# The slot table, the return of the first image and the opening of the scans in a four-layer network on one core

## The chip, the cores and the metric

The kernel runs on one core of a Trainium2 chip. A core has TensorE (PE; its weight loads are shown as PEld), VectorE (DVE), ScalarE (ACT), GpSimd (POOL) and SyncE (SP), which issues DMAs. The metric is the device time of one execution in microseconds (us); lower is better.

## The reference, cut to what matters

Four layers, each added to its input `x` (2 images of 128 channels, 56x56) after a group norm: agent attention, a 3x3 convolution, a mixture of experts over 2x2 patches, and a two-directional Mamba scan over the rows.

```
x = x + _L0_conv_ref(_gn(x), ...)      # attention
x = x + _L1_conv_ref(_gn(x), ...)      # 3x3 convolution
x = x + _L2_conv_ref(_gn(x), ...)      # experts
x = x + _L3_conv_ref(_gn(x), ...)      # scans
...
logits = xp @ router_w                  # xp: 1568 tokens of 512
topv, topi = jax.lax.top_k(softmax(logits), 2)
for e in range(8):
    val, g = jnp.split(xp @ w1[e], 2, axis=-1)
    out = out + gate[:, e:e+1] * ((val * sigmoid(g)) @ w2[e])
...
xc = silu(conv_b + causal conv of 4 taps)            # Mamba, each direction
dt = softplus(...); h = exp(dt * A) * h + dt * u * B; y = h . C
```

All data is float32.

## The kernel before

**Slot table.** Each token goes to two experts. The kernel sorts the 2 x 1568 pairs into tiles of 128 slots (`SLOTS`), each tile of one expert; up to 32 tiles (`TILES`) are possible, 25 are sure (`self.fewest`), and this input has 28. At the end of `route`, `inv` gets, for each slot and tile, the token and its share. It is one product over tokens: `is_slot` (112 tokens x 128 slots, 0 or 1) is the stationary side, `what` (112 tokens x 64: token and share for 32 tiles) the moving one; 14 token blocks for each of the two choices, 28 matmuls that add into one PSUM bank (L1292). DVE builds `is_slot` and `what` in two rooms that lie in buffers of the weights.

**Experts.** `run` (from L1315) loops over tiles. For tile j, SP reads the expert's number into a register (`expert`, L1324) and issues `w1` (4 MB, L1331) and `w2` (2 MB, L1336); each has two buffers. POOL gathers the tile's 128 tokens (`xr`, indirect DMA, L1306, four buffers). `up` transposes them on PE (`xr_ps`, L1354), DVE copies them to `xs_c` (L1356), and 64 matmuls (L1365) fill four banks `h_ps`, a quarter each; ACT takes the sigmoid (`sg`, L1375), DVE multiplies to `ht` (L1377). `down` of the tile before (8 matmuls `o_ps`, L1385, ACT's `ot`, L1388, and a DMA to `os`) follows `up`. A matmul of float32 shows as two records. Outside blocks of `manual_schedule` the framework's scheduler orders each engine's instructions by its own estimates; `issue_after(ins)` makes what the block issues on the engine of `ins` come after `ins`.

**Return of image 0.** Tiles 0 to 19 hold all of image 0 (`self.ahead` is 20). `arrive` is a generator: `combine` gathers, for each of 7 token blocks, two rows per token from `os` (`g0`, `g1`, L1306 again), DVE adds them (L1461), PE transposes the sum (`y_ps`, L1464), DVE adds it onto `x` (L1437) and takes statistics (L88); then come three stages of the group norm (L100, `gn_ps` L104 and L116) and the roots. `lead` blocks are gathered ahead. `run` calls `next(beside)` at tile 20 three times (`LEAD`), and from tile 21 on at every `spot()`, after each half of `up` and after each `down`; a `spot` holds PE's part behind the last matmul traced (`traced`). After tile 24 the rest of the generator runs, and then a `Switch` on the number of further tiles, here 3.

**Opening of the scans.** `mamba_pair` keeps its own order on all engines. An agenda books stages by steps; steps below 0 prepare direction f of block 0: `conv`, `silu`, `low`, `step`, `log`, `softplus`, `weigh`, `send_steps`. In the same steps the generator `second` brings image 1 back from all 28 tiles and takes its norm. Each `next` of it gathers one block and works on it at once (`lead` 0). Its PSUM banks are the wide ones of `dA` (`wide_bank`). Then come 448 units: ACT makes `dA` (L1876), POOL `dBu` (L1887), DVE scans (L1906), and DVE or POOL multiplies by C.

Of the kernel before, what the change touches and what calls it, by code (L numbers as in the profile page):

```python
# [8 lines left out]
F32 = mybir.dt.float32  # L9
# [1004 lines left out]
class PatchExperts:  # L1014
# [15 lines left out]
    def route(self, dram, wpool, conv):  # L1030
# [9 lines left out]
        with tc.tile_pool(name="l2_route", bufs=1) as one, tc.tile_pool(  # L1040
# [12 lines left out]
            four = one.tile([P, 32], F32, name="four")  # L1053
            nc.vector.tensor_reduce(four, net.ident.rearrange("p (q e) -> p e q", q=4), AX.X, ALU.add)
            shape = [T, nt, experts]

# [192 lines left out]
            self.slots = []  # L1249
            inv = ps.tile([P, 512], F32, name="inv", tag="tr")  # L1250
            rooms = [
# [3 lines left out]
            for n, room in enumerate(rooms):  # L1255
# [27 lines left out]
                for some in (range(per), range(per, nt)):  # L1283
                    ts = slice(some[0], some[-1] + 1)
                    nc.vector.tensor_tensor(
                        is_slot[:, ts, :],
                        slot_of.unsqueeze(1).to_broadcast([T, per, SLOTS]),
                        low[:, ts].unsqueeze(2).to_broadcast([T, per, SLOTS]),
                        ALU.is_equal,
                    )  # L1290
                    for t in some:
                        nc.tensor.matmul(  # L1292
                            inv[:, : 2 * TILES],
                            is_slot[:, t, :],
                            what[:, t].rearrange("t h j -> t (h j)"),
                            start=n == 0 and t == 0,
                            stop=n == 1 and t == nt - 1,
                        )

            self.whom = keep.tile([P, TILES], I32, name="whom")  # L1300
            nc.vector.tensor_copy(self.whom, inv[:, :TILES])
# [13 lines left out]
    def run(self, wpool, work, ps, beside):  # L1315
# [11 lines left out]
        downs = [wpool.tile([P, nj, 512], F32, name="w2", tag="w2") for _ in range(2)]  # L1327

        def up_weights(j, e):
            w1 = ups[j % 2]  # L1330
            nc.sync.dma_start(w1, w1s[e].rearrange("o c q f -> (o c) q f"))  # L1331
            return w1
# [5 lines left out]

        traced = [None]

        def spot():
            with net.tc.issue_after(traced[0]):
                next(beside, None)

# [5 lines left out]
        def up(j, w1, xr):  # L1350

            tp = ps.tile([P, 512], F32, name="xr_ps", tag="tr")
            for q in range(4):
                nc.tensor.transpose(tp[:, q * P : (q + 1) * P], xr[:, q * P : (q + 1) * P], net.ident)  # L1354
            xc = work.tile([P, 4, SLOTS], F32, name="xs_c", tag="xs_c")
            nc.vector.tensor_copy(xc.rearrange("c q s -> c (q s)"), tp)  # L1356
            ht = work.tile([P, nj, SLOTS], F32, name="ht", tag="ht")
            for c in range(2):
                parts = []
                for part in (1, 0):  # L1360
                    h_ps = ps.tile([P, 512], F32, name="h_ps", tag="h", bufs=4)
                    for i in range(4):
                        f0 = part * hidden + (4 * c + i) * P
                        for q in range(4):
                            mm = nc.tensor.matmul(  # L1365
                                h_ps[:, i * SLOTS : (i + 1) * SLOTS],
                                w1[:, q, f0 : f0 + P],
                                xc[:, q, :],
                                start=q == 0,
                                stop=q == 3,  # L1370
                            )
                    traced[0] = mm.ins
                    parts.append(h_ps)
                sg = work.tile([P, 4 * SLOTS], F32, name="sg", tag="sg")
                nc.scalar.activation(sg, parts[0], AF.Sigmoid)  # L1375
                to = ht[:, 4 * c : 4 * c + 4, :].rearrange("k j s -> k (j s)")
                nc.vector.tensor_mul(to, parts[1], sg)  # L1377
                if self.ahead + 1 < j + c < self.fewest + c:
                    spot()
            return ht  # L1380
# [13 lines left out]
        for j in range(self.fewest):  # L1394
            e = expert(j)
            w1, w2 = up_weights(j, e), down_weights(j, e)
            ht = up(j, w1, gather(j))
            if last is not None:
                down(*last)
            last = (j, ht, w2)  # L1400
            if j == self.ahead:
                for _ in range(LEAD):
                    next(beside)
            elif j > self.ahead:
                spot()
        for _ in beside:
# [75 lines left out]

LEAD = 3

# [95 lines left out]
def arrive(net, combine, b, gathered, bank, banks, pool, norms, lead=0):  # L1580
    nc = net.nc
    yield from combine(b, gathered, bank, lead)
    got = []
    for stage in net.norm_stages(b, banks, "mm", got.append):
        fetch = stage()
# [10 lines left out]
def mamba_pair(net, out, wts, combine, keep, norms):  # L1596
# [19 lines left out]
    with ExitStack() as ctx:  # L1616
# [15 lines left out]
        def wide_bank(name):  # L1632
            return ps.tile([P, 1024], F32, name=name, tag="dA", bufs=2)

        class Banks:
            def tile(self, shape, dtype, name, tag):
                return wide_bank(name)[:, :512]

# [100 lines left out]
        class Half:  # L1739
# [5 lines left out]

            def conv(self, m):
                w = self.w
# [11 lines left out]
                if m == 0:  # L1759
                    self.xc = work.tile([P, 2, BLK], F32, name="xc", tag=f"xc{w.d}", bufs=1 if w.d == "f" else 2)  # L1760
                return lambda: nc.scalar.activation(
                    self.xc[:, m, :], pm[:, :BLK], AF.Identity, bias=w.conv_b[:, m : m + 1]
                )

# [187 lines left out]
        for n, blk in enumerate(blocks):  # L1952
# [3 lines left out]
            if n == 0:  # L1956

                book(at + 1, blk.norm)
                book(at + 3, lambda f=f: f.conv(0))
                book(at + 4, lambda f=f: f.conv(1), tag="c")  # L1960
                book(at + 6, lambda f=f: silu(f, None))
                book(at + 7, f.low)
# [8 lines left out]
                for i, (h, m) in enumerate(((f, 0), (f, 1), (b, 0), (b, 1))):  # L1971
                    book((1, 4, 5, 13)[i], lambda h=h, m=m: h.gate(m))
                book(at + 17, lambda b=b: b.conv(0))
                book(at + 17, lambda b=b: b.conv(1), tag="c")
                book(at + 19, lambda b=b: silu(b, None))
                for m in range(2):
# [66 lines left out]
        with tc.manual_schedule(engines={E.PE, E.Activation, E.DVE, E.Pool, E.SP}):  # L2043
            nc.scalar.preload_act_table_set(EXP_LN)
            second = arrive(net, combine, 1, gathered, wide_bank, ps_of_norms, keep, norms)
            first = min(agenda)
            for step in range(first, 0):
                run(step)
                for _ in range((0, 0, 0, 2, 0, 1, 1, 0, 1, 1, 1, 1, 0, 1, 1, 1)[step - first] if step - first < 16 else 1):
                    next(second, None)  # L2050
                fetch(step + 1)
            for _ in second:
                pass
        with tc.manual_schedule(engines={E.PE, E.Activation, E.DVE, E.Pool, E.SP}):
# [5 lines left out]
            for n, (h, u) in enumerate(units):  # L2060
# [13 lines left out]
                if done:  # L2074
                    done.pop().close()
                waiting.append((h, u))

                quota = 0 if u == 3 and n > 3 else 2 if u == 7 and n > 7 else 1
# [125 lines left out]
```

## Time and profile before

| | |
|---|---|
| median of 3 runs | 3031.53 us (3031.18 to 3033.45) |
| the profiled execution | 3033.16 us, its span 3031.1 us |
| busy, share of the span | PE 89%, DVE 72%, ACT 61%, POOL 48% |
| attention and convolution | to about 1000 us |
| `inv` matmuls | 1011.82 to 1024.0 us |
| experts, first `h_ps` to last `ot` | 1036.2 to 1677.7 us |
| first scan | 1717.74 us |
| weights `w1` (4 MB), issue to landing | median 20.4 us, 12.5 to 23.1 |
| weights `w2` (2 MB), issue to landing | median 10.9 us, 9.3 to 30.0 |
| `os` written | 28 x 256 KB, median 7.9 us to landing |
| gathers (L1306), issue to landing | median 7.8 us, 3.3 to 14.0 |

A line of a timeline has the start, the duration, engine, source line, operation, what it writes and reads, and a count of instructions that follow each other; brackets hold the idle time of the engine before them and what ended it. "issue" is a wait for nothing that the profile names.

### The profile page before, as it was taken

The numbers are of one execution on the slowest core, as the hardware profiler recorded it, in microseconds if no ns is written. First come the engines' busy times: TensorE is split into PE (matmuls) and PEld (weight loads), VectorE is DVE, ScalarE is ACT, GpSimd is POOL, SyncE is SP. The second block draws the span as 40 slices with busy tenths as digits, with TensorE's granted clock in tenths as the row PEclk, the third lists the DMA queues.
The fourth block names the chain that finished last, engine by engine and source line by source line (L and its number), as shares of the span: only waits on it lengthen the run. The fifth ranks groups of instructions, "written<-read, shape, count | busy, mean of one in ns | idle before, by whom it ended". The sixth has DMA issues, their size and how long they took to land. (4 is left out here: it accounts for less than half of the span.)

```text
span 3031.1 us, 39355 instructions
## 1 busy us (share of the span) xinstructions
PE 2697.4 (89%) x14924; PEld 1283.4 (42%) x14924; DVE 2184.0 (72%) x1854; ACT 1853.7 (61%) x2944; POOL 1450.5 (48%) x801
## 2 busy tenths in 40 slices
PE   7999999999998799999898778888888888888874
PEld 3333333333335688788777323333333333233321
DVE  5978998999886301010120589999999999999996
ACT  5778788778751100000001488888888888888884
POOL 3000010010322100000100589999999999999995
PEclk9999999999999799999999799899899999999987
DMA  1000000000002668788875554465555565545460
GB/s 55 1 1 1 1 1 1 1 1 1 1 1 60 263 272 318 314 310 321 303 279 206 129 125 116 114 148 130 120 118 121 117 147 127 127 116 120 115 148 22
DMA packets 157934, 369.32 MB, mean 122 GB/s; under 512 B 25156, under 2 KB 114980, under 8 KB 154132
## 3 DMA queue, kind: packets, MB, share of 16 engines
q1 hardware_dynamic: 135744, 339.30, 37.5%
q0 software_dynamic: 5520, 15.62, 1.6%
q10 hardware_dynamic: 16452, 11.61, 1.2%
q8 instruction: 122, 2.00, 0.3%
q14 instruction: 96, 0.79, 0.1%
HBM read 297.89 MB, written 17.20 MB: 104 GB/s over the span
## 5 line engine op out<-in xcount | busy, mean ns | idle before, releaser
L1887 POOL TENSOR_TENSOR dBu<-dtu,Bs 128x896 f32<-128x896 f32 x448 | 921.3, 2094 | 14.4 <-DMA dtu<-sp_u 10.5
L1906 DVE TENSOR_TENSOR_SCAN h<-dA,dBu 128x896 f32<-128x896 f32 x448 | 882.3, 2009 | 28.2 <-ACT dA L1876 24.8
L620 ACT ACTIVATE ex<-sc 128x896 f32<-128x896 f32 (+1 forms) x700 | 602.6, 918 | 124.7 <-PE sc L617 113.4
L1928 PE MATMUL y<-h,both 128*64 128x448 f32 x1792 | 468.2, 615 | 82.2 <-POOL h L1915 74.9
L627 DVE TENSOR_TENSOR ex_sum<-ex_sum,ex 128x1792 f32<-128x1792 f32 (+1 forms) x238 | 492.6, 2070 | 35.3 <-ACT ex L620 21.3
L1365 PEld LDWEIGHTS h_ps<-xs_c,w 128*128 128x128 f32 x3584 | 406.5, 193 | 28.6 <-ACT ot L1388 15.4
L1365 PE MATMUL h_ps<-xs_c,w 128*128 128x128 f32 x3584 | 409.9, 277 | 9.0 <-issue 9.0
L617 PE MATMUL sc<-q,k 32*128 32x448 f32 (+1 forms) x2800 | 403.6, 587 | 3.6 <-ACT ex L620 2.9
L1917 DVE TENSOR_TENSOR h<-h,c_ps 128x1792 f32<-128x1792 f32 (+1 forms) x168 | 326.6, 1944 | 26.9 <-ACT c_ps L1894 10.1
L635 PE MATMUL av<-ex,va 128*32 128x448 f32 (+1 forms) x2800 | 334.3, 552 | 0.1
L582 POOL TENSOR_TENSOR a_e<-a_e,a_inv 112x784 f32<-112x784 f32 x14 | 41.6, 2973 | 584.0 <-ACT ex L620 394.5
L1377 DVE TENSOR_TENSOR ht<-h_ps,sg 128x512 f32<-128x512 f32 x56 | 38.5, 691 | 391.8 <-PE h_ps L1365 339.7
L1876 ACT ACTIVATE dA<-dt,f_A 128x448 f32<-128x448 f32 x448 | 282.7, 636 | 50.7 <-DVE h L1906 39.7
L1876 ACT ACTIVATE dA<-dt,b_A 128x448 f32<-128x448 f32 x448 | 282.8, 635 | 33.1 <-DVE h L1906 24.2
L1928 PEld LDWEIGHTS y<-h,both 128*64 128x64 f32 x1792 | 118.9, 147 | 354.8 <-issue 212.6
L1306 POOL DMA_INDIRECT xr<-xd,whom x28 | 28.1, 1004 | 493.3 <-PE xr_ps L1354 449.3
L1915 POOL TENSOR_TENSOR h<-h,Cs 128x1792 f32<-128x1792 f32 (+1 forms) x70 | 252.5, 3608 | 6.9 <-PE sp_ps L1841 3.4
L617 PEld LDWEIGHTS sc<-q,k 32*128 32x128 f32 (+1 forms) x2800 | 137.7, 181 | 230.1 <-issue 132.5
L1375 ACT ACTIVATE sg<-h_ps 128x512 f32<-128x512 f32 x56 | 33.4, 597 | 310.0 <-PE h_ps L1365 309.9
L1385 PE MATMUL o_ps<-w,ht 128*128 128x512 f32 x448 | 204.4, 601 | 1.2 <-DVE ht L1377 1.2
L1388 ACT ACTIVATE ot<-o_ps,share 128x512 f32<-128x512 f32 x28 | 19.2, 687 | 255.5 <-PE o_ps L1385 255.5
L625 DVE TENSOR_TENSOR ex_sum<-ex 128x1792 f32<-128x1792 f32 x56 | 114.4, 2043 | 54.5 <-ACT ex L620 54.4
(342 smaller groups left out, 3006.7 us busy)
## 6 DMA issues: line engine op xcount, KB each, us to landing
w<-in_L_conv_w_dram SPq DMA_DIRECT2D x28, 4096.0 KB, 20.4
w<-in_L_conv_w_dram SPq DMA_DIRECT2D x28, 2048.0 KB, 10.9
Bs<-far SPq DMA_DIRECT2D x56, 896.0 KB, 7.7
Cs<-far SPq DMA_DIRECT2D x448, 112.0 KB, 2.9
dtu<-sp_u SPq DMA_DIRECT2D x108, 224.0 KB, 3.8
dt<-dt SPq DMA_DIRECT2D x108, 224.0 KB, 4.9
os<-ot ACTq DMA_DIRECT2D x28, 256.0 KB, 7.9
xd<-xt SPq DMA_DIRECT2D x14, 224.0 KB, 2.7
```

Of the source, the lines that this page charges most:

```text
L617: nc.tensor.matmul(sc[:size, j, :BLK], self.m.k[rows, at : at + size], self.q[rows, :], start=True, stop=True)
L620: nc.scalar.activation(ex[:size, 2 * g : 2 * g + 2, :], sc[:size, :, :BLK], AF.Exp, scale=scale)
L627: nc.vector.tensor_add(self.total[g][:size], self.total[g][:size], ex[:size])
L635: nc.tensor.matmul(self.av[rows, :BLK], self.m.va[:size, i, rows], self.ex[i][:size, h, :], start=i == 0, stop=i == STEPS - 1,)
L1365: mm = nc.tensor.matmul(h_ps[:, i * SLOTS : (i + 1) * SLOTS], w1[:, q, f0 : f0 + P], xc[:, q, :], start=q == 0, stop=q == 3,)
L1385: mm = nc.tensor.matmul(o_ps, ht[:, i, :], w2[:, i, :], start=i == 0, stop=i == nj - 1)
L1876: nc.scalar.activation(self.dA[u][:, r * BLK : (r + 1) * BLK], self.dt2[:, m, r, :], AF.Exp, scale=self.w.A[:, j, 2 * m + r : 2 * m + r + 1],)
L1887: nc.gpsimd.tensor_tensor(self.dBu[u], self.dtu2[:, m], self.B[:, j, :].unsqueeze(1).to_broadcast(shape), ALU.mult)
L1906: nc.vector.tensor_tensor_scan(hf, af, bf, 0.0, ALU.mult, ALU.add)
L1915: nc.gpsimd.tensor_tensor(h4, h4, self.C[j].unsqueeze(1).to_broadcast(shape), ALU.mult)
L1917: nc.vector.tensor_tensor(h4, h4, self.c_ps[:, :BLK].unsqueeze(1).to_broadcast(shape), ALU.mult)
L1928: nc.tensor.matmul(self.y[r * H : (r + 1) * H, m, :BLK], both, self.hc[j][:, m, r, :], start=False, stop=j == PAIRS - 1)
```

## The change

There are three parts.

**Slot table by halves.** The two sides of the product change places: `what` (64 columns) is stationary, `is_slot` moves, and the result `turned` has tile and kind along partitions. Even token blocks add into partitions 0 to 63, odd ones into 64 to 127. The copy `table` is then multiplied by `fold` (two identities of 64 on top of each other), which adds the halves and turns the table.

```
+ fold = one.tile([P, 2 * TILES], F32, name="fold")
+ nc.vector.tensor_add(fold, net.ident[:, : P // 2], net.ident[:, P // 2 :])
...
+     g = t % 2 * 2 * TILES
      nc.tensor.matmul(
-         inv[:, : 2 * TILES],
-         is_slot[:, t, :],
-         what[:, t].rearrange("t h j -> t (h j)"),
-         start=n == 0 and t == 0,
-         stop=n == 1 and t == nt - 1,
+         turned[g : g + 2 * TILES, :SLOTS],
+         what[:, t].rearrange("t h j -> t (h j)"),
+         is_slot[:, t, :],
+         start=n == 0 and t < 2,
+         stop=n == 1 and t >= nt - 2,
      )
+ table = one.tile([P, SLOTS], F32, name="table")
+ nc.vector.tensor_copy(table, turned[:, :SLOTS])
+ inv = ps.tile([P, 512], F32, name="inv", tag="tr")
+ nc.tensor.matmul(inv[:, : 2 * TILES], table, fold, start=True, stop=True)
```

**Experts.** The PE work of tiles 1 to 3 stays behind the first quarter of tile 0, and SP's work of each tile (register loads included) behind the first or second fetch of `w1`. `LEAD` is 5. The return's steps are at fixed quarters of tiles 22 to 24, and DVE's part is held behind the last `xs_c` or `ht` (`shaped`).

```
+ turns = {2: (1, 3, 4), 3: (0, 1, 2, 3, 4, 4), 4: (0, 1)}
+ def spot(j, at):
+     if j < self.fewest:
+         for _ in range(turns.get(j - self.ahead, ()).count(at)):
+             with net.tc.issue_after(traced[0]), net.tc.issue_after(shaped[0]):
+                 next(beside)
...
      traced[0] = mm.ins
+     starts.append(mm.ins)
      parts.append(h_ps)
+     spot(j, 2 * c + 1 - part)
...
- if self.ahead + 1 < j + c < self.fewest + c:
-     spot()
...
+ if 0 < j < 4:
+     behind.enter_context(net.tc.issue_after(starts[0]))
+ if j > 0:
+     behind.enter_context(net.tc.issue_after(fetches[min(j - 1, 1)]))
+ with behind:
      e = expert(j)
      w1, w2 = up_weights(j, e), down_weights(j, e)
      ht = up(j, w1, gather(j))
...
- elif j > self.ahead:
-     spot()
+ spot(j, 4)
...
- LEAD = 3
+ LEAD, LEAD2 = 5, 3
```

**Opening.** The first block's `conv` writes silu straight from its bank; what is left of `silu(None, None)` is the preload of the table for exp and ln. Image 1's generator gathers three blocks first (`LEAD2`); its first sum stands in the step of `low`. Its norm moves into the loop over units, where it takes the banks of the agenda's stages.

```
- return lambda: nc.scalar.activation(
-     self.xc[:, m, :], pm[:, :BLK], AF.Identity, bias=w.conv_b[:, m : m + 1]
- )
+ return lambda: nc.scalar.activation(self.xc[:, m, :], pm[:, :BLK], as_, bias=w.conv_b[:, m : m + 1])
...
+ book(at + 3, lambda f=f: f.conv(0, AF.Silu))
+ book(at + 4, lambda f=f: f.conv(1, AF.Silu), tag="c")
+ book(at + 6, lambda: silu(None, None))
...
- nc.scalar.preload_act_table_set(EXP_LN)
- second = arrive(net, combine, 1, gathered, wide_bank, ps_of_norms, keep, norms)
+ second = arrive(net, combine, 1, gathered, back_bank, ps_of_norms, keep, norms, LEAD2)
  for step in range(first, 0):
      run(step)
-     for _ in range((0, 0, 0, 2, 0, 1, 1, 0, 1, 1, 1, 1, 0, 1, 1, 1)[step - first] if step - first < 16 else 1):
-         next(second, None)
+     for _ in range((LEAD2, 0, 0, 0, 0, 0, 1, 0, 1, 2, 1, 1, 1, 1)[step - first] if step - first < 14 else 0):
+         next(second)
      fetch(step + 1)
- for _ in second:
-     pass
+ opening = False
...
      waiting.append((h, u))
+     next(second, None)
```

Direction b of block 0 is booked with `AF.Silu` in the same way.

More of the change, by code (lines that the diff above doesn't have):

```diff
@@ L1249, in route @@
             self.slots = []
-            inv = ps.tile([P, 512], F32, name="inv", tag="tr")
+            turned = ps.tile([P, 512], F32, name="turned", tag="tr")
             rooms = [
@@ L1327, in run @@
         downs = [wpool.tile([P, nj, 512], F32, name="w2", tag="w2") for _ in range(2)]
+        starts, fetches = [], []
         def up_weights(j, e):
             w1 = ups[j % 2]
-            nc.sync.dma_start(w1, w1s[e].rearrange("o c q f -> (o c) q f"))
+            dma = nc.sync.dma_start(w1, w1s[e].rearrange("o c q f -> (o c) q f"))
+            fetches.append(dma.ins)
             return w1
@@ L1337, in down_weights @@
             return w2
[L1339 to L1343, printed above, removed]
+        traced, shaped = [None], [None]
+        turns = {2: (1, 3, 4), 3: (0, 1, 2, 3, 4, 4), 4: (0, 1)}
[4 more added lines that the diff above has]
+                        next(beside)
         def gather(j):
@@ L1355, in up @@
             xc = work.tile([P, 4, SLOTS], F32, name="xs_c", tag="xs_c")
-            nc.vector.tensor_copy(xc.rearrange("c q s -> c (q s)"), tp)
+            shaped[0] = nc.vector.tensor_copy(xc.rearrange("c q s -> c (q s)"), tp).ins
             ht = work.tile([P, nj, SLOTS], F32, name="ht", tag="ht")
@@ L1376, in up @@
                 to = ht[:, 4 * c : 4 * c + 4, :].rearrange("k j s -> k (j s)")
-                nc.vector.tensor_mul(to, parts[1], sg)
-                if self.ahead + 1 < j + c < self.fewest + c:
-                    spot()
+                shaped[0] = nc.vector.tensor_mul(to, parts[1], sg).ins
             return ht
@@ L1394, in run @@
         for j in range(self.fewest):
-            e = expert(j)
-            w1, w2 = up_weights(j, e), down_weights(j, e)
-            ht = up(j, w1, gather(j))
+            behind = ExitStack()
+            if 0 < j < 4:
[3 more added lines that the diff above has]
+            with behind:
+                e = expert(j)
+                w1, w2 = up_weights(j, e), down_weights(j, e)
+                ht = up(j, w1, gather(j))
             if last is not None:
@@ L1583, in arrive @@
     got = []
-    for stage in net.norm_stages(b, banks, "mm", got.append):
+    for n, stage in enumerate(net.norm_stages(b, banks, "mm", got.append)):
         fetch = stage()
@@ L1633, in wide_bank, with back_bank @@
             return ps.tile([P, 1024], F32, name=name, tag="dA", bufs=2)
+        opening = True
+        def back_bank(name):
+            return wide_bank(name) if opening else mm(name)
         class Banks:
             def tile(self, shape, dtype, name, tag):
-                return wide_bank(name)[:, :512]
+                return back_bank(name)[:, :512]
         ps_of_norms = Banks()
@@ L1744, in __init__, with conv @@
                 self.dA, self.dBu, self.hc, self.C = {}, {}, {}, {}
-            def conv(self, m):
+            def conv(self, m, as_=AF.Identity):
                 w = self.w
@@ L1958, in mamba_pair @@
                 book(at + 1, blk.norm)
-                book(at + 3, lambda f=f: f.conv(0))
-                book(at + 4, lambda f=f: f.conv(1), tag="c")
-                book(at + 6, lambda f=f: silu(f, None))
+                book(at + 3, lambda f=f: f.conv(0, AF.Silu))
+                book(at + 4, lambda f=f: f.conv(1, AF.Silu), tag="c")
+                book(at + 6, lambda: silu(None, None))
                 book(at + 7, f.low)
@@ L1972, in mamba_pair @@
                     book((1, 4, 5, 13)[i], lambda h=h, m=m: h.gate(m))
-                book(at + 17, lambda b=b: b.conv(0))
-                book(at + 17, lambda b=b: b.conv(1), tag="c")
-                book(at + 19, lambda b=b: silu(b, None))
+                book(at + 17, lambda b=b: b.conv(0, AF.Silu))
+                book(at + 17, lambda b=b: b.conv(1, AF.Silu), tag="c")
+                book(at + 19, lambda: silu(None, None))
                 for m in range(2):
```

## The prediction

> **What bounds the kernel now.** I read the page's rows by time slice first, then the busy time by stage, then the waits of PE, and then the timelines of single engines where PE or DVE stands still.
>
> ```profile
> 1036.00:1500.00 464.00, 464.00 (x3205) 380.91 (x3205) 42.71 (x62) 41.30 (x65) 24.07 (x25) 1.00 0.80 313
> 1500.00:1680.00 180.00, 157.36 (x965) 121.87 (x965) 29.11 (x72) 17.68 (x26) 11.77 (x12) 0.93 0.62 229
> 1680.00:1720.00 40.00, 30.80 (x81) 15.27 (x80) 20.68 (x55) 17.27 (x28) 21.57 (x26) 0.79 0.79 191
> 1720.00:3031.00 1311.00, 1077.97 (x3587) 407.51 (x3585) 1229.16 (x699) 1076.00 (x1924) 1237.74 (x585) 0.90 0.50 119
> ```
>
> Columns: stretch, its length, busy us of PE, PEld, DVE, ACT, POOL, then PE's granted clock, DMA share, GB/s. The experts (1036 to 1680) are PE's: 464 of 464 us until 1500, 157 of 180 after. From 1720 on the scans hold DVE and POOL at 94% each, so a microsecond won before 1720 should arrive at the end. All the edits lie between 1006 and 1750. Where PE loses its time there:
>
> ```profile
> PE y_ps L1464 <- DVE g L1461: 13.1, 4, 9.2
> PE h_ps L1365 <- issue: 9.0, 1, 9.0
> PE xr_ps L1354 <- DMA xr<-xd,whom: 8.0, 1, 8.0
> ```
> ```profile
> 1011.82 12.18 PE L1292 MATMUL inv<-room 112*128 112x64 f32 x56 [4.54 <-DVE tile_f L1267]
> 1032.05 4.36 PE L1354 MATMUL xr_ps<-ident,xr 128*128 128x128 f32 x16 [8.05 <-DMA xr<-xd,whom]
> 1036.20 14.80 PE L1365 MATMUL h_ps<-xs_c,w 128*128 128x128 f32 x128
> ...
> 1510.15 1.02 PE L1464 MATMUL y_ps<-ident,g 112*128 112x112 f32 x4 [9.16 <-DVE g L1461]
> 1510.97 8.07 PE L1385 MATMUL o_ps<-w,ht 128*128 128x512 f32 x14
> ...
> 1602.02 16.87 PE L1365 MATMUL h_ps<-xs_c,w 128*128 128x128 f32 x128 [9.03 <-issue]
> ...
> 1692.51 3.21 PE L1781 MATMUL low_ps<-xc,f_xp_t 128*40 128x448 f32 x4
> ```
> ```profile
> 1509.40 0.69 DVE L1461 TENSOR_TENSOR g<-g,g 112x512 f32<-112x512 f32 x1 [23.04 <-DMA g<-os,at_i]
> ...
> 1601.23 0.69 DVE L1356 COPY xs_c<-xr_ps 128x512 f32<-128x512 f32 x1 [5.76 <-issue]
> ...
> 1717.74 2.01 DVE L1906 TENSOR_TENSOR_SCAN h<-dA,dBu 128x896 f32<-128x896 f32 x1
> ```
>
> Start, duration, what ran, count, and in brackets the idle time before it. After each halt the same work runs slower for a while: 14 `o_ps` records take 8.07 us at 1510.97 and 6.17 in undisturbed tiles; 128 `h_ps` records 16.87 against 14.53. So a halt is paid twice.
>
> **A. Slot table, and the way into the experts.** Before, 56 `inv` records take 12.18 us, 0.215 each, at a granted clock of 0.54. Now each has 64 columns of weights and 128 moving columns, and even and odd blocks use different halves of PSUM's partitions. The nearest row is `y<-h,both` (64 weight columns, halves alternating): 12 records in 2.48 us, the last lasting 0.54, so starts are (2.48 - 0.54)/11 = 0.176 apart. Whole-width `conv_ps` of the same 448 columns needs 6.35/16 = 0.397. Halves overlap, then: 0.44 of the whole. The lower bound is 0.215 x 0.44 = 0.095 a record; the load of 64 columns against 128 (137 to 190 ns) gives 0.155; no overlap at all gives 0.215. I take 0.125: 56 x 0.125 = 7.0 us, 5.2 saved. Added on the path: the copy `table` (0.28, as L142's 128x128 copies), a matmul of two records (0.45, as `tot` L1176) and two hand-overs (0.1 each): +0.9. DVE is no limit: its last `what` ends at 1015.7. Net -4.3; bounds -6.0 and +0.9. `fold` is one 0.2 us DVE operation some hundred microseconds earlier, beside convolutions.
>
> The Trainium skill, "TensorE: Matmul & The Clock Gate", section "The mechanism", speaks against this: a weight load overlaps a running matmul only if its row group differs, and halves of columns share all row groups. Here `h_ps` loads are busy 380.91 of 464 us under matmuls that fill all 464 (both on all 128 rows), so this trace disagrees. By the rule a record would be load plus matmul, 0.155 + 0.125 = 0.28, and the kernel 56 x 0.155 = 8.7 us slower than I forecast.
>
> The gathers of `xr` follow the table: issued at 1024.52, transposed at 1032.05, and still 7.5 us. `w1` of tile 0 must not be late instead. It was issued at 1014.47, behind 14 register loads from 1005.6 on (0.63 each); now two stand ahead of it: about 1007, 12.5 us to landing in that window, 1019.5. Then 4 transposes stand before the first `h_ps` and not 16. The first `xs_c` copy was over at 1033.9, so `h_ps` can start at 1034.0 and not 1036.20: -2.2. The other 12 are now paid at full clock, 3 x 0.44 = +1.3, and `h_ps` starts with a colder PE, as at 1602.02: 16.87 - 14.80 = +2.1 (0 at the least). **A = -4.3 - 2.2 + 1.3 + 2.1 = -3.1** (-6.9 to +2.1).
>
> **B. The return of image 0.** In tile 21 PE came to the first `y_ps` before the gathers had landed. Now the sums and transposes of block 0 stand behind the second quarter of tile 22 (about 1515), and its data was there at 1509.4; every later block has a quarter or more. So these halts go: 9.16, with 8.07 - 6.17 = 1.90 of slow clock; then 1.92 before the `xr_ps` at 1544.43, with 1.15 (3.03 - 1.88) and 0.56 (7.88 - 7.32) after it. The third halt is the norm's: DVE did `gn` work until 1595.47, passed the Switch 5.76 us later, and copied `xs_c` only at 1601.23. Now the two `gn_ps` matmuls stand behind the first and second quarter of tile 24, and DVE's last work ahead of the Switch is `ht`. Measured from tile 24's first `h_ps`: sigmoid of the second half would be at 11.0, but ACT's two table loads, two roots, `pad` and the load back (3 x 1.28 + 0.4 + 0.8, from 7.7) put it at 14.1, `ht` ends at 15.5, and with the 5.76 DVE is through at 21.3; the transposes that it copies end at 21.8. So 9.03 + 2.34 go, with 0.5 to spare. Sum 26.06.
>
> What is late next: `w1` of tile 22, issued at 1485.79, landed 23.1 us later, at 1508.9; PE, no longer halted, wants it at 1486.46 + 14.53 + 6.0 + 0.44 + 0.86 = 1508.3. Eight gathers beside it had cost 23.1 - 20.4 (the median) = 2.7; two to four more may be under way before it lands: +1.2 in all. If the tile after it is late as well and PE goes cold each time, 2 x (2.2 + 2.3) = 9. POOL's four extra gathers (1.3 each) push only `xr` of tiles 26 and 27, wanted 100 us later. **B = -26.1 + 1.2 = -24.9** (-26.1 to -17).
>
> **C. The opening of the scans.** ACT had `xc` ready at 1687.0, but `low_ps` stood behind three `y_ps` groups that waited for gathers: 1692.51. Now it stands first, and silu reads the bank: two operations of 0.63 after one table load, without the second load and the 0.95 pass, so `xc` is there at 1684.8: `low_ps` 7.6 earlier. Not all of that is kept: three `y_ps` groups now stand ahead of the first `sp_ps`, and the fourth block's sum still ends at 1694.1 (POOL needs 1.3 us a gather). `sp_ps` starts near 1695.2 and not 1700.64: -5.4. `dt`, its DMAs and the first scan follow, less what the second half loses to its own queue: -4.7. Then ACT pays for silu in the second direction: its two halves now have a scan factor `dA` between them, so four table loads stand where two did, 2 x 1.28 = +2.6, less the 0.95 pass; and the second norm's five DVE operations now stand among scans 1 to 4, waiting for PE and ACT. Up to the fourth scan little is left (-1), but DVE waits 5.09 us for ACT's `c_ps` at 1748.77 in any case, and that hangs on ACT's and PE's chain (`low`, `dt_ps`, `sp_ps` of direction b), which is earlier by 4.7 + 0.95 - 2.6 = 3.1 at silu's end, and by some 0.6 more where the norm's `ir` operations no longer stand in between. **C = -3.7** (-7.6; +3 if ACT sets the end and the norm chain's 4.3 us, 1713.36 to 1717.67, falls between scans).
>
> The Trainium skill, "ScalarE: Activation LUTs", section "What ACT_TABLE_LOAD costs", adds 1.38 us of drain to each 1.28 us load. Here the load at 1721.65 ends at 1722.93 and the next operation starts at 1722.95: no drain is seen. By the page, C would be 2.8 us worse.
>
> **The sum** is made against the profiled execution: span 3031.1 and 2.1 around it, 3033.16; the median of the runs, 3031.53, lies 1.6 below. -3.1 - 24.9 - 3.7 = -31.7: 3001.5 there, 3000 as a median.
>
> **The rivals.**
> (1) The Switch costs what it costs: DVE's 5.76 and SP's 7.5 us past it (1591.28 to 1598.75) are the branch's own, and if `ht` or ACT ends a little later than I reckon, the halt stays. Against it: PE's own way past is 0.52 and DVE came to it 10 us late. It takes back 11.4: 3011.
> (2) The weights' queue becomes the bound of tiles 22 to 25, for PE now runs 26 us faster through the same bytes: 311 GB/s in undisturbed tiles, 333 at most with gathers. It takes back 8: 3008. For it: only 1.6 us of slack in an undisturbed tile; against it: just two tiles have gathers in them.
> (3) Slower: the pinned sums hold DVE's queue. Each stands ahead of an `ht`, and behind `ht` come PE's banks of `h_ps`. If gathers land later than about 22 us after their issue, PE halts at each of 9 places (7 sums, 2 norm steps), 2.2 of wait and 2.3 of cold clock each: +40, 3040. It decides above 31.7/9 = 3.5 us a place. The longest landing in the trace is 14.0, against it.
> (4) The halts move but don't shrink, within 0.2%: 3031.
>
> **How the numbers follow.** The forecast 3000, own range 2992 to 3007: 66%. Rival 1: 14%. Rival 2: 11%. Rival 3: 6%. Rival 4: 3%. The range 2991 to 3014 takes in the forecast's bounds and the first two rivals. Faster by over 0.2% (6 us, about what can be told from no change) 0.91, within 0.03, slower 0.06.
>
> **What would show it.** A: `turned` in 6 to 9 us, first `xr_ps` near 1028, first `h_ps` near 1030. B: no idle over 2 us ahead of `y_ps` L1483, `xs_c` of tile 25 within 1 us of its transposes. C: `low_ps` directly after `xc`, first scan about 35 us after the end of the last `ot` (40.0 before: 1677.7 to 1717.74). I am wrong if PE waits on `w` in tiles 22 to 25 for more than 5 us, if the Switch still holds DVE past the transposes, or if DVE's waits for `dA` and `c_ps` in the first 40 us of the scans grow.

## The result and the profile after

The changed kernel takes 3026.93 us (median of 20 runs, 3021.0 to 3032.73), the kernel before 3033.61 beside it (20 runs); the ratio is 0.9979, interval 0.9972 to 0.9986. It is 6.7 us faster, against 31.7 forecast, and lies outside the range. The profiled execution took 3025.19 us, its span 3023.5.

The busy time by stage of the changed kernel, with the columns of the first view of the prediction:

```profile
1500.00:1665.00 165.00, 158.68 (x1023) 125.14 (x1022) 28.97 (x72) 18.31 (x27) 15.96 (x16) 0.99 0.72 268
1665.00:1705.00 40.00, 27.09 (x82) 13.82 (x80) 17.64 (x46) 15.28 (x24) 21.63 (x26) 0.83 0.81 195
```

The experts end at 1663 instead of 1677, with PE busy 159 of 165 us (157 of 180 before) at full clock. That gain is there; it must have been lost elsewhere. The waits of PE between 1010 and 1740, changed kernel (what waited, what ended it, sum, times, longest):

```profile
PE xr_ps L1368 <- DMA xr<-xd,whom: 13.0, 1, 13.0
...
PE h_ps L1379 <- DMA w<-in_L_conv_w_dram: 4.3, 2, 3.5
```

The wait for the first gather grew from 8.0 to 13.0, and `h_ps` now waits for weights. Where these stand in PE's timeline:

```profile
1015.30 3.26 PE L1295 MATMUL turned<-room 112*64 112x128 f32 x28 [4.54 <-DVE tile_f L1269]
1019.24 3.26 PE L1295 MATMUL turned<-room 112*64 112x128 f32 x28 [0.68 <-DVE room L1282]
...
1036.59 1.09 PE L1368 MATMUL xr_ps<-ident,xr 128*128 128x128 f32 x4 [13.02 <-DMA xr<-xd,whom]
1038.52 17.46 PE L1379 MATMUL h_ps<-xs_c,w 128*128 128x128 f32 x128 [0.84 <-DVE xs_c L1370]
...
1515.73 7.38 PE L1379 MATMUL h_ps<-xs_c,w 128*128 128x128 f32 x64 [0.71 <-DMA w<-in_L_conv_w_dram]
...
1542.78 5.44 PE L1379 MATMUL h_ps<-xs_c,w 128*128 128x128 f32 x32 [3.55 <-DMA w<-in_L_conv_w_dram]
...
1686.04 0.99 PE L1483 MATMUL y_ps<-ident,g 112*128 112x112 f32 x4 [7.38 <-DVE g L1480]
1686.83 1.72 PE L1863 MATMUL sp_ps<-sp_e,ident 128*128 128x448 f32 x2
```

DVE's, in the norm of image 1 and at the fourth scan, before the change:

```profile
1712.20 0.16 DVE L109 TENSOR_TENSOR gn_d<-gn_mv,gn_mean 128x1 f32<-128x1 f32 x1
1712.40 0.22 DVE L110 SCALAR_TENSOR_TENSOR gn_q<-gn_d,gn_mv 128x1 f32<-128x1 f32 x1
...
1715.48 1.69 DVE L69 TENSOR_TENSOR ir_t<-ir_v,gn_rstd 128x1 f32<-128x1 f32 x1 [1.97 <-ACT gn_rstd L68]
...
1729.03 2.02 DVE L1906 TENSOR_TENSOR_SCAN h<-dA,dBu 128x896 f32<-128x896 f32 x1 [0.38 <-ACT dA L1876]
```

And in the changed kernel, from the first scan on:

```profile
1700.97 2.02 DVE L1928 TENSOR_TENSOR_SCAN h<-dA,dBu 128x896 f32<-128x896 f32 x1 [1.43 <-POOL dBu L1909]
...
1707.35 2.02 DVE L1928 TENSOR_TENSOR_SCAN h<-dA,dBu 128x896 f32<-128x896 f32 x1 [4.12 <-ACT dA L1898]
1712.95 0.16 DVE L107 COPY gn_mean<-gn_ps 128x1 f32<-128x1 f32 x1 [3.58 <-PE gn_ps L104]
1713.15 1.03 DVE L109 TENSOR_TENSOR gn_d<-gn_mv,gn_mean 128x1 f32<-128x1 f32 x1
1714.21 3.88 DVE L110 SCALAR_TENSOR_TENSOR gn_q<-gn_d,gn_mv 128x1 f32<-128x1 f32 x1
1718.02 2.01 DVE L1928 TENSOR_TENSOR_SCAN h<-dA,dBu 128x896 f32<-128x896 f32 x1
...
1722.28 2.00 DVE L70 SCALAR_TENSOR_TENSOR ir_t<-ir_t,gn_rstd 128x1 f32<-128x1 f32 x1
1724.32 2.00 DVE L71 SCALAR_TENSOR_TENSOR gn_rstd<-ir_t,gn_rstd 128x1 f32<-128x1 f32 x1
1726.24 2.01 DVE L1928 TENSOR_TENSOR_SCAN h<-dA,dBu 128x896 f32<-128x896 f32 x1
```

The first scan stands 37.9 us behind the last `o_ps` (40.8 before), but the fourth stands 25.3 behind the first (11.3 before). Six operations of the norm, on one element per partition, now take 1.0 to 3.9 us each; before the change five of them took 0.16 to 0.22, and one, L69, 1.69: the trace of before held the sign already, for L69 ended there at 1717.17, when an operation of POOL's ended (`dBu`, 1715.09 to 1717.16).

From such lines the span splits at four marks: the first table matmul, the first `h_ps` of tile 4, the end of the last `o_ps`, and the end.

| stretch | before | after | change | forecast |
|---|---|---|---|---|
| start to table | 1011.8 | 1015.3 | +3.5 | 0 |
| table to tile 4 (A) | 103.9 | 107.2 | +3.2 | -3.1 |
| tile 4 to last `o_ps` (B) | 561.2 | 540.6 | -20.6 | -24.9 |
| last `o_ps` to end (C) | 1354.2 | 1360.4 | +6.3 | -3.7 |

The first row is no part of the change: over the kernels below it lies between 1009.9 and 1015.3, whether they have the new table or not (x1_pins_only, without it, has 1015.1).

### The profile page after: what moved, and what is told of

The parts are those of the page before. It is cut to its first block, busy times and chain, and to the rows that moved or that the text cites. A ratio compares the mean times of both kernels' runs of the same rounds, so it can differ in the third digit from the quotient of the medians.

```text
span 3023.5 us, 39364 instructions
## 1 busy us (share of the span) xinstructions
PE 2685.7 (89%) x14926; PEld 1271.7 (42%) x14926; DVE 2192.9 (73%) x1856; ACT 1855.9 (61%) x2943; POOL 1451.1 (48%) x801
## 5 line engine op out<-in xcount | busy, mean ns | idle before, releaser
L627 DVE TENSOR_TENSOR ex_sum<-ex_sum,ex 128x1792 f32<-128x1792 f32 (+1 forms) x238 | 492.7, 2070 | 37.9 <-ACT ex L620 23.8
L1939 DVE TENSOR_TENSOR h<-h,c_ps 128x1792 f32<-128x1792 f32 (+1 forms) x168 | 326.6, 1944 | 25.3 <-ACT c_ps L1916 7.7
L1937 POOL TENSOR_TENSOR h<-h,Cs 128x1792 f32<-128x1792 f32 (+1 forms) x70 | 252.8, 3611 | 11.7 <-issue 8.6
## 6 DMA issues: line engine op xcount, KB each, us to landing
Cs<-far SPq DMA_DIRECT2D x448, 112.0 KB, 2.9
```

The lines of the kernel that those rows point to most:

```text
L627: nc.vector.tensor_add(self.total[g][:size], self.total[g][:size], ex[:size])
L1937: nc.gpsimd.tensor_tensor(h4, h4, self.C[j].unsqueeze(1).to_broadcast(shape), ALU.mult)
L1939: nc.vector.tensor_tensor(h4, h4, self.c_ps[:, :BLK].unsqueeze(1).to_broadcast(shape), ALU.mult)
```

## The experiments

All are timed against the kernel before on the same chip.

| kernel | median us | before us | ratio and interval |
|---|---|---|---|
| x1_pins_only | 3018.58 | 3032.95 | 0.9948, 0.9935 to 0.9961 |
| x2b_old_sp | 3020.25 | 3032.95 | 0.9952, 0.9939 to 0.9965 |
| x3_old_opening | 3014.07 | 3032.95 | 0.9930, 0.9917 to 0.9942 |
| x4_norm_open | 3020.12 | 3032.95 | 0.9952, 0.9939 to 0.9965 |
| x5_both_old | 3011.20 | 3034.13 | 0.9927, 0.9914 to 0.9941 |
| x6_sums_late | 3023.03 | 3034.13 | 0.9960, 0.9947 to 0.9974 |
| x7_one_port | 3016.64 | 3034.13 | 0.9945, 0.9932 to 0.9959 |
| x8_silu_bank | 3009.73 | 3034.13 | 0.9924, 0.9910 to 0.9937 |
| x9_bs_late | 3019.57 | 3034.05 | 0.9956, 0.9943 to 0.9970 |
| x10_best | 3004.87 | 3034.05 | 0.9911, 0.9897 to 0.9925 |
| x11_lead3 | 3006.83 | 3034.05 | 0.9914, 0.9900 to 0.9927 |
| x12_two_gathers | 3000.95 | 3032.32 | 0.9899, 0.9884 to 0.9914 |
| x13_best_lead3 | 3003.48 | 3032.32 | 0.9914, 0.9900 to 0.9928 |

### Which part gave the time back: x1_pins_only and x3_old_opening

x1_pins_only is the kernel before with the pinned sums (`turns`, `shaped`, `LEAD = 5`) alone.

> The kernel before with part B alone (pinned return of image 0, five blocks gathered ahead); slot table, order of SP and opening as before. My theory: the two traces put the gain in B (-20.6 us from the first matmul of tile 21 to the end of the experts) and losses in A (+3) and C (+6 to +9), so this kernel is about 20 us faster than the kernel before, ratio 0.993, and faster than the changed kernel by 10 or more. Rival: B's gain is an artefact of where one trace was cut, and the pins alone give what the whole change gives, 5 to 8 us, ratio 0.998.

x3_old_opening is the changed kernel with `silu`, the turns of `second` and the norm of image 1 as before:

```
- book(at + 3, lambda f=f: f.conv(0, AF.Silu))
+ book(at + 3, lambda f=f: f.conv(0))
...
- second = arrive(net, combine, 1, gathered, back_bank, ps_of_norms, keep, norms, LEAD2)
+ second = arrive(net, combine, 1, gathered, wide_bank, ps_of_norms, keep, norms)
...
+ for _ in second:
+     pass
```

> The changed kernel with the opening of the scans as before (image 1's blocks gathered one at a time, its norm ahead of the scans, silu as a pass of its own, one table preload). My theory: the new opening costs 6 to 10 us, so this kernel is 13 to 17 us faster than the kernel before, ratio 0.995, and the stretch from the last expert matmul to the sixth scan is as before. Rival: the new opening is a gain and the 6 us are lost elsewhere in the scans; then it is no faster than the changed kernel, ratio 0.998 or above.

The pins alone win 15.8 us (0.0052 of 3033), less than the 20 expected but twice what the whole change wins; their trace has 542.5 us from tile 4 to the last `o_ps`, 18.7 less than before. With table and order of the weights added, and the opening old, it is 21.2, more than expected. So the changed opening is what costs: 0.9979 - 0.9930 is 14.9 us, and 25.3 us between first and fourth scan become 10.1. The stretch from the last `o_ps` to the end, 1356.2 us against 1360.4, says less: over the six traces with the old opening it lies between 1348.6 and 1356.6. The part that the opening decides is seen better at the twentieth scan: it stands 107.1 us behind the last `o_ps` before the change, 117.8 in the changed kernel and 109.0 in x3_old_opening; from there to the end the traces take 1239 to 1247 us, whatever the opening.

### The order of the first weights: x2b_old_sp

The changed kernel without the line that puts SP's work behind a fetch; PE's pin stays.

```
- if j > 0:
-     behind.enter_context(net.tc.issue_after(fetches[min(j - 1, 1)]))
```

> The changed kernel, but SP reads its 14 registers ahead of the first fetch of weights, as before; slot table by halves and the later transposes stay. My theory: the first gathers are slow in the changed kernel because the 4 MB fetch of tile 1's first weights runs beside them and no longer tile 0's second weights; here they run beside the latter again and land within 8 us of their issue (12.5 in the changed kernel, 7.5 before), the first matmul of the experts comes 4 to 5 us earlier after the table is ready, and the kernel is 3 to 5 us faster than the changed one, ratio to before 0.9965. Rival: the gathers are slow for another reason (their place right after the table, the colder PE), landing stays above 11 us and the time stays at 0.998.

The first gather is on PE 7.17 us after its issue and not 12.50:

```profile
1025.90 1.09 PE L1368 MATMUL xr_ps<-ident,xr 128*128 128x128 f32 x4 [7.69 <-DMA xr<-xd,whom]
```

The stretch from table to tile 4 takes 100.7 us: 3.2 less than before the change, where 3.1 was forecast. By the ratios the kernel is 8.2 us faster than the changed one, more than the 3 to 5 expected. What gathers run beside shows in the DMA queues between 1032 and 1034 us, as packets, MB and share of the 16 engines; the first gather is still under way in the changed kernel then, and before the change those behind it are. Before the change:

```profile
q0 software_dynamic: 129, 0.44, 56.0%
q1 hardware_dynamic: 169, 0.37, 49.8%
```

The changed kernel:

```profile
q1 hardware_dynamic: 27, 0.88, 103.0%
q0 software_dynamic: 19, 0.08, 9.5%
```

q0 holds the gathers, q1 the weights. Before, q1's packets are of 0.37 MB / 169 = 2.2 KB (`w2`); after, of 33 KB (`w1` of tile 1, issued at 1022.53, which moves as soon as `w2` of tile 0 is through). In both cases the queues get about the same number of packets, so the bytes go to the queue with the larger ones: the gathers get 0.08 MB in 2 us and not 0.44. The order of SP decides which of the two they meet: in the eight kernels with SP's order of before the gather needs 7.2 to 7.5 us, in the seven with the new one 11.5 to 12.5.

The Trainium skill, "DMA: Bandwidth & Descriptors", section "Queues, rings and completion order", states this: each DMA engine takes a packet from one queue, then one from the next. It would have warned against the forecast's 7.5 us, since it makes the weights' packet size part of a gather's landing time.

### The norm of image 1 between the scans: x4_norm_open and x7_one_port

x4_norm_open finishes the generator `second`, norm included, ahead of the scans; all else is as changed.

> The changed kernel, but the norm of image 1 is finished ahead of the first scan. My theory: in the loop over units the norm's small VectorE operations wait for POOL's operations (0.16 us each in the opening, 1 to 3.9 in the loop, some 11 us in all); ahead of the scans they take 0.2 each, the first scan comes 3 to 4 us later, the fourth 4 to 6 us earlier, and the kernel is 3 to 6 us faster than the changed one, ratio to before 0.9965. Rival: ACT's four table loads set the pace between the first and fifth scan; then the fourth scan comes no earlier and the time stays at 0.998 or gets worse.

It is 8 us faster than the changed kernel by the ratios. The first scan comes 13 us later (51.1 behind the last `o_ps`; 3 to 4 later expected), but the four scans then start within 5.8 us, so that the fourth comes 6.4 us earlier. The rival, ACT's table loads, would have kept the fourth scan where it was. The small operations are slow here too, against what was expected, for example:

```profile
1701.36 2.02 DVE L109 TENSOR_TENSOR gn_d<-gn_mv,gn_mean 128x1 f32<-128x1 f32 x1
1703.41 1.99 DVE L110 SCALAR_TENSOR_TENSOR gn_q<-gn_d,gn_mv 128x1 f32<-128x1 f32 x1
```

So it is not the place among scans that makes them slow. In the changed kernel's timeline of POOL stands what ran beside L109 and L110 (1.03 and 3.88 us above):

```profile
1703.96 10.20 POOL L1909 TENSOR_TENSOR dBu<-dtu,Bs 128x896 f32<-128x896 f32 x5 [3.02 <-DMA dtu<-sp_u]
1714.12 3.96 POOL L1937 TENSOR_TENSOR h<-h,Cs 128x1792 f32<-128x1792 f32 x1
```

L109 ends at 1714.18 and L110 at 1718.09, each when POOL's operation ends. The copies L107 and L66, which read PSUM, take 0.13 to 0.16 in the same place. x7_one_port writes the same six operations so that the second tile comes in as a column of scalars:

```
- nc.vector.tensor_sub(d, mv[:, 0:1], mean)
- nc.vector.scalar_tensor_tensor(q, d, d, mv[:, 1:2], ALU.mult, ALU.add)
+ nc.vector.tensor_scalar(d, mv[:, 0:1], mean, None, ALU.subtract)
+ nc.vector.tensor_scalar(q, d, d, mv[:, 1:2], ALU.mult, ALU.add)
```

> The changed kernel with the norm's six small VectorE operations that read two tiles of SBUF (lines 69, 70, 71, 109, 110, 1610) written as tensor_scalar with the second tile as a column of scalars; same place, same values, same number of operations. My theory: these 128x1 operations took 1.0 to 3.9 us in the changed kernel because an operation with two SBUF tensor inputs waits out the GpSimd operation that runs; as tensor_scalar they take 0.2 us each, some 10 us of DVE time between the second and the fourth scan goes, the fourth scan starts within 20 us of the first (25.3 in the changed kernel), and the time falls by 3 to 8 us, ratio 0.9955 to 0.997. Rival: they wait because GpSimd is busy at all, or for their inputs: durations stay over 1 us and the ratio at 0.998.

Its DVE timeline, the same part of the norm, with POOL in `dBu` until 1716.46 and in `h` until 1720.38:

```profile
1715.25 0.16 DVE L112 COPY gn_mean<-gn_ps 128x1 f32<-128x1 f32 x1 [3.57 <-PE gn_ps L109]
1715.45 0.21 DVE L114 TENSOR_SCALAR gn_d<-gn_mv,gn_mean 128x1 f32<-128x1 f32 x1
1715.70 0.27 DVE L115 TENSOR_SCALAR gn_q<-gn_d,gn_mv 128x1 f32<-128x1 f32 x1
1715.89 2.01 DVE L1933 TENSOR_TENSOR_SCAN h<-dA,dBu 128x896 f32<-128x896 f32 x1
...
1719.73 0.21 DVE L72 TENSOR_SCALAR gn_rstd<-ir_t,gn_rstd 128x1 f32<-128x1 f32 x1
```

POOL is as busy as before, and the operations take 0.15 to 0.27 us. First to fourth scan falls from 25.3 to 16.6 us, and the time by 10.3 (0.9979 to 0.9945; the intervals leave 6 to 15), more than expected. The twentieth scan comes 5.8 us earlier behind the last `o_ps` (112.0, for 117.8). The rival (POOL being busy at all, or late inputs) is out.

The Trainium skill, "SBUF — State Buffer", section "Who interferes with whom", has the rule: a VectorE operation with two SBUF inputs reads the second through an interface that it shares with GpSimd, and whoever comes second waits for the whole of the other's operation. The trace agrees, with up to 3.88 us for an operation of 0.22.

### Silu from the bank: x8_silu_bank

The old order of image 1, with only the silu changed:

```
- book(at + 3, lambda f=f: f.conv(0))
+ book(at + 3, lambda f=f: f.conv(0, AF.Silu))
...
- book(at + 6, lambda f=f: silu(f, None))
+ book(at + 6, lambda: silu(None, None))
```

> The changed kernel with the order of before for the second image in the opening (its sums and its norm ahead of the first scan, two of the wide banks for them) but the silu read from the bank in both convolutions. It differs from x3_old_opening by the silu alone. My theory: silu from the bank saves about 1.4 us ahead of low_ps and costs 2.6 us of table loads where the second direction's convolution falls among the dA, so that the first scan comes 1 to 2 us earlier and the time is that of x3_old_opening within 3 us, ratio 0.9925 to 0.994. Rival: the table loads among the dA are what the changed opening lost its 13 us by: ratio 0.996 or more, the four table loads within 6 us and second to fourth scan over 20 us behind the first as in the changed kernel (25.3) instead of 10 (x3_old_opening).

The first scan comes 40.5 us behind the last `o_ps` (41.7 in x3_old_opening), then DVE waits 7.56 us for `dA` behind ACT's table loads, and first to fourth scan takes 13.4 us instead of 10.1. Yet the time is that of x3_old_opening (0.9924 against 0.9930). So the rival is out, and silu from the bank, its table loads included, neither wins nor costs anything that can be measured here.

### Bs beside the gathers: x6_sums_late and x9_bs_late

In the changed kernel `Bs` (two transfers of 896 KB) is issued at 1675.47, in the middle of image 1's gathers; before, at 1699.03, behind them. The sum of the fourth block then waits 6.3 us for its gathers, and `sp_ps` stands behind it. x6_sums_late gathers four blocks ahead and puts the sums of blocks 3 to 6 behind `sp_ps`:

```
- (LEAD2, 0, 0, 0, 0, 0, 1, 0, 1, 2, 1, 1, 1, 1)
+ (LEAD2, 0, 0, 0, 0, 0, 1, 0, 1, 1, 0, 0, 0, 2, 2, 1)
```

> The changed kernel with four gathers ahead instead of three and the second image's sums of blocks 3 to 6 asked of PE and DVE behind the step weights (sp_ps) of the first direction instead of ahead of them. My theory: sp_ps waits on PE behind a y_ps whose gather lands 9 us after its issue, because it runs beside the two Bs transfers; with the sums behind it sp_ps starts 6 us earlier or more (17 us or less after the first convolution instead of 23) and the first scan comes 33 us or less after the last o_ps instead of 38; the time falls by 3 to 8 us against the changed kernel, ratio 0.9955 to 0.997. Rival: the scans wait for the transfers of dt and dtu and for the norm's place, whatever the sums do: the first scan comes earlier but the fourth does not, ratio 0.998 as the changed kernel.

`sp_ps` comes 21.7 us behind the first convolution's start (23.0 in the changed kernel, 17 expected), since the third sum, still ahead of it, now waits 5.7 us. The first scan is not earlier, 42.0 us behind the last `o_ps`: ACT waits 9.15 us with `dA` for DVE's late sums, whose banks `dA` uses. The time, 0.9960, is 5.8 us below the changed kernel, but the two intervals touch; the mechanism expected did not bring it, and what did, if anything, is open. x9_bs_late moves the transfer instead (on top of x7_one_port): it is issued from ACT's queue behind the second `sp_w`, at 1684.49.

```
- nc.sync.dma_start(self.B[half], src[s].unsqueeze(0).to_broadcast([H, PAIRS, BLK]))
+ queue.dma_start(self.B[half], src[s].unsqueeze(0).to_broadcast([H, PAIRS, BLK]))
...
+ book(at + 11, lambda: f0.spread_b(nc.scalar))
```

> x7_one_port with the two Bs transfers of the first direction's opening issued from ACT's queue behind the second sp_w instead of from SP right behind far, so that they start some 8 us later, when the second image's gathers have mostly landed. My theory: the third and fourth sums then no longer wait for gathers beside Bs (6.6 us of DVE idle for DMA g in x7_one_port becomes under 2), sp_ps starts 17 us or less after the first convolution's first matmul (23.5 in x7_one_port), the first scan comes 3 us or more earlier after the last o_ps, and the ratio falls from 0.9945 to about 0.993. Rival: Bs itself then lands last and dBu waits for it: the first scan stays within 2 us of 41.5 after the last o_ps and the ratio at 0.9945.

DVE's and POOL's timelines in x9_bs_late:

```profile
1702.84 2.02 DVE L1937 TENSOR_TENSOR_SCAN h<-dA,dBu 128x896 f32<-128x896 f32 x1 [9.87 <-POOL dBu L1918]
```
```profile
1700.74 12.23 POOL L1918 TENSOR_TENSOR dBu<-dtu,Bs 128x896 f32<-128x896 f32 x6 [8.43 <-DMA dtu<-sp_u]
```

`sp_ps` is 6.6 us earlier (18.9 behind the first convolution's start; in x7_one_port it is 25.5, not the 23.5 that the expectation names), but POOL now waits 8.43 us for `dtu`, now issued right behind `Bs`, and the first scan stands 42.6 us behind the last `o_ps` (41.5 in x7_one_port). The ratio is 0.9956 against 0.9945. The rival holds: what the chain of `sp_ps` wins it loses again in its own transfers.

### Both repaired: x5_both_old and x10_best

x5_both_old joins the edits of x2b_old_sp and x3_old_opening.

> The changed kernel with the opening of before and with the fetches of the expert weights in the order of before ahead of the first turn (only PE stays pinned there), so that the slot table, the halves and the pinned sums stay. My theory: the opening as changed costs some 13 us and the gathers beside the 4 MB weights of the second expert some 5, and the two add: x3_old_opening (ratio 0.9930) less about 4 us, ratio 0.9917, near 3010 us; first gather to first xr_ps under 8 us, first table matmul to h of tile 4 near 101 us. Rival: what the first turn gains is lost again where tiles 1 to 4 wait for their weights, which then start later: table to h of tile 4 stays over 104 us and the ratio at 0.993.

Table to tile 4 takes 101.1 us as expected, 4.3 less than in x3_old_opening; of the time only 0.9 us are seen (0.9927), inside the interval, so the 4 us are shown in the trace and not in the timing. x10_best adds silu from the bank and the norm as `tensor_scalar`.

> Slot table, halves and pinned sums of the changed kernel, SP's order of before ahead of the first turn, second image's sums and norm ahead of the first scan as in before, silu from the bank, and the norm's small operations as tensor_scalar. My theory: x8_silu_bank (0.9924) with the first gathers off the second expert's weights (up to 4 us, of which x5_both_old kept 1) and about 1 us of the norm: ratio 0.9910 to 0.9920. Rival: the parts no longer add, 0.9925 as x8_silu_bank and x5_both_old.

0.9911: 27 us faster than the kernel before and 20.6 (0.0068 of 3033) faster than the changed one.

### The weights of tiles 22 and 23: x11_lead3, x12_two_gathers, x13_best_lead3

x11_lead3 is x5_both_old with `LEAD = 3`; the sums keep their turns.

> x5_both_old with three blocks gathered ahead on the last always-run tiles instead of five, the sums at the same turns. My theory: the burst of ten gathers at tile 21 lies beside the weights of tiles 22 and 23 and makes their first matmuls wait (0.7 and 3.6 us in the changed kernel); with six gathers the two waits fall under 2 us together, and h of tile 4 to the last o_ps becomes 2 to 4 us shorter than in x5_both_old. Rival: the 1 MB moved is the same and only shifts: tiles 24 and 25 wait instead, or the sums wait for their gathers; no gain, ratio 0.9927.

Tile 4 to last `o_ps` takes 540.5 us (540.9), and `h_ps` waits 3.55 us for weights (4.24), where under 2 were expected: the burst of ten gathers is at most a small part of the cause. x12_two_gathers, also on x5_both_old, gathers only blocks 0 and 1 of image 0 and sums these two again for the others.

```
+ if b == 0 and k > 1:
+     return kept[k % 2]
```

> x5_both_old with the rows of the first image's blocks 2 to 6 not gathered: their sums run at the same turns, on the tiles that blocks 0 and 1 were gathered into, so that the first image's result is not that of the reference; the bytes of ten of the fourteen gathers are left out. My theory: the two waits of h_ps for w1 on the last always-run tiles (4.2 us in x5_both_old) are the gathers' bytes beside 6 MB of weights a tile, however they are spread (x11_lead3 kept 3.5): they fall under 1.5 us, and h of tile 4 to the last o_ps takes 537 to 538.5 us instead of 540.9. Rival: the weights are late by the fetch order or by their own landing time at the new pace of the tiles: waits stay over 3 us, 540 us or more.

In its timeline of PE the first quarters of the tiles that waited are:

```profile
1505.74 7.38 PE L1379 MATMUL h_ps<-xs_c,w 128*128 128x128 f32 x64 [1.18 <-DMA w<-in_L_conv_w_dram]
...
1528.96 3.81 PE L1379 MATMUL h_ps<-xs_c,w 128*128 128x128 f32 x32
```

The second wait and its cold clock (5.28 us for 32 records in x5_both_old, 3.81 here) are gone, and the stretch takes 536.3 us, 4.5 less; the time falls by 8.5, more than the stretch explains. So the gathers' transfers make the weights late, for the most part however they are spread; the rival is out.

> x10_best with three blocks gathered ahead instead of five in the first image's return. My theory: nothing more, since x11_lead3 showed the stretch h of tile 4 to the last o_ps unchanged (540.5 against 540.9 us): ratio 0.991 as x10_best, within 0.0013. Rival: the 0.0013 between x5_both_old and x11_lead3 was real and adds: ratio 0.990 or less.

x13_best_lead3 has 0.9914, as x10_best (0.9911): in the time, the smaller lead is worth nothing. In the traces it does a little. `w1` of tile 23 lands 27.2 us after its issue in x13_best_lead3, 28.3 in the changed kernel and 20.4 in x12_two_gathers. The first quarter of tile 23 waits 1.8 us in x13_best_lead3 and 2.2 in x11_lead3, against 3.5 to 4.5 in all eleven kernels that gather five blocks ahead. After the wait of 1.8 it runs at full pace (3.81 us), after that of 2.2 it does not (5.40), and tile 4 to the last `o_ps` takes 538.5 us in x13_best_lead3 (541.5 in x10_best).

## Why the prediction was wrong, point by point

**A, the table.** Right in its own terms: 28 + 28 records of `turned` in 3.26 us each, 0.116 a record (0.125 taken, at a granted clock of 0.50 in both kernels, which I had read as 0.54), table to first gather 8.8 us instead of 12.7 (-3.9; -4.3 taken), transposes to first `h_ps` -2.2 as taken, cold clock +2.7 (+2.1 taken). The step that failed is "The gathers of `xr` follow the table ... and still 7.5 us": it took 12.5. I had looked at whether `w1` of tile 0 came in time, and not at which transfer its earlier start would put beside the gathers. x2b_old_sp, with that step undone, gives the forecast sum. The Trainium skill, "TensorE: Matmul & The Clock Gate", section "The mechanism", has a weight load overlap a running matmul only where the row group differs (or, as it also says there, where the load goes to the background weight buffer). By the first of these I had estimated 0.28 a record, with a scaled record time (0.155) put in for a load; a load lasts 0.23 in this trace, and 28 of them with their matmuls fit into 3.26 us, so loads do overlap here.

**B, the return.** The halts went as forecast: no `y_ps` of tiles 22 to 24 waits in the changed kernel, and `xs_c` of tile 25 runs at 1589.65, 0.1 us behind its transposes, so the Switch (rival 1) does not hold it. The term that was mis-sized is "+1.2 in all" for late weights: 0.71 + 3.55 of waiting and 5.44 - 3.75 of cold clock are 5.9. Rival 2 happened in part, within the 9 I named as its end; x12_two_gathers shows it as the gathers' bytes: I had counted the few gathers beside the `w1` of tile 22, and the larger wait was that of tile 23, whose `w1` took 28.3 us to land. The terms that I named for ACT's second sigmoid add up to 12.7 and not to 14.1, but nothing hung on it (`ht` ended at 15.8, for 15.5). Rival 3 did not happen.

**C, the opening.** `low_ps` does stand directly behind `xc`, and here the rightness ends. "`sp_ps` starts near 1695.2 and not 1700.64" failed: from the first convolution's start it stands 23.0 us behind (22.9 before). `Bs`, moved forward with `low`, shares the DMA engines with the gathers: with `Bs` later, in x9_bs_late, `sp_ps` stands 18.9 us behind instead of 25.5. What `far` adds was not tried. I counted the edit's instructions on PE, ACT and DVE and not the DMAs that hang on `low`. And "the second norm's five DVE operations now stand among scans 1 to 4" was given no price but waits for PE and ACT ("up to the fourth scan little is left (-1)"). The norm's six small operations took 1.0 to 3.9 us each, 11.7 in all, and the fourth scan stands 63.2 us behind the last `o_ps`, 52.1 before: +11.1 for that -1. x7_one_port shows that this was most of the 15 us that the opening lost: 10 by the ratios, 6 by the twentieth scan; the rest (0.9945 against 0.9930) is inside the intervals. The term for ACT's table loads (+2.6) was not needed (x8_silu_bank); four loads of 1.28 us stand among the `dA`, the operation behind each starts 0.01 to 0.02 us after its end, and no drain is seen.

**The sum.** -31.7, with +6.3 in A, +4.3 in B, +10.0 in C and +3.5 ahead of the change, gives the -7.6 of the spans. None of the three signs of being wrong that I had named came up: PE waits 4.3 us for `w`, not over 5, the Switch holds nothing, and in the first 40 us of the scans DVE waits 4.1 us for `dA` and `c_ps` (10.4 before). None of the three looks at the first gather, at `sp_ps` or at how long the norm's operations run; of what was to show the forecast right, the first `xr_ps` (1036.6, for 1028) and the first scan (37.2 us behind the last `ot`, for 35) missed. Rival 4's number (3031) was nearer than mine, but nothing of its reason happened. That x10_best is 27 us faster than the kernel before says that most of the forecast's gain was there to be had, though not by the new opening; the change gave it back in places that I had not looked at.

## What to carry to other kernels

Where an edit lets a transfer start earlier, ask which other transfer it will now lie beside, and how large that one's packets are: here a gather beside 33 KB packets needed 11.5 to 12.5 us instead of 7.2 to 7.5. Where small VectorE work is moved into a stretch in which GpSimd computes, write it with one SBUF tensor input (PSUM, or the second as a column of scalars), or count up to a whole GpSimd operation for each instruction. Undo the parts of a combined change one at a time: here the whole won 6.7 us and one part alone 15.8.

## What the runs showed of the hardware that was not expected

Two DMA queues share by packets: 129 against 169 packets of 3.4 and 2.2 KB, and 19 against 27 where one queue's are 33 KB, so 0.08 against 0.88 MB in the same 2 us. A 128x1 VectorE operation with two SBUF inputs took 0.16 to 0.22 us alone and up to 3.88 beside GpSimd's multiply; as `tensor_scalar`, 0.21 to 0.27 in the same place. Matmuls with 64 weight columns that alternate between the halves of PSUM's partitions take 0.116 us a record at 128 moving columns and a granted clock of 0.50. One kernel's executions differ by more than several parts of this change are worth: the 20 runs of the kernel before lie between 3025.59 and 3037.54.
